# An attention block with a mixture of experts: first group normed tile by tile, routing pairs counted earlier, the last stage's first rows loaded into left buffers

## The chip, the cores and the metric

The kernel runs on one core of a Trainium2 chip. The metric is device time in microseconds (us), taken around the whole execution of the program. A core has TensorE (PE, with its weight load PEld), VectorE (DVE), ScalarE (ACT), GpSimd (POOL) and SyncE (SP). SP, ACT and POOL can also issue DMAs; an engine executes its instructions, DMA issues among them, in the order in which the program gives them.

## The reference

The input x is 4 sequences of 1024 rows of 512 floats. Everything is float32.

```python
xn = layernorm(x)                                  # no gain, no bias
q, k, v = xn @ Wq.T + bq, xn @ Wk.T + bk, xn @ Wv.T + bv      # 16 heads of 32
scores = q @ k.T / sqrt(32), causal, - slope[h] * |i - j|
attn = softmax(scores) @ v @ Wo.T + bo

logits = xn @ gate_w.T                             # 8 experts
topw, sel = top_k(softmax(logits), 2); topw /= topw.sum()
g, u = split(xn @ w1[e].T)                         # 352 wide each
expert_out[e] = (silu(g) * u) @ w2[e].T
ffn = sum over the 2 chosen experts of topw * expert_out

return x + attn + ffn
```

## The kernel before, in words

Rows are worked on in 32 tiles of 128. There are three phases on TensorE's one in-order stream.

**First phase (norm and routing, the first 105 us).** A loop of 12 steps i runs a pipeline over 8 groups of four tiles (LG = 4). `load_pair` fetches x two tiles at a time on SP's queue (the first two pairs are split in tiles between SP and ACT). `norm_stats(g)` makes mean and variance of the four tiles on DVE, `norm_root(g)` one square root for the four on ACT, `norm_rows(g)` one reciprocal on DVE and then the rows themselves: tile 0 (and tile 2 in group 0) on DVE, tile 1 on ACT, the others on POOL. `norm_turn(g)` transposes each tile on PE (L327) and ACT copies it out of PSUM (L328). `norm_gate` (L339) makes the gate's logits, `norm_top`, `norm_pick` and `norm_rank` choose the two experts of each row and count within a tile. Between these steps the loop takes pieces of the first projections from the list `proj`: four q and k pieces of the first attention unit and eight v pieces, each 8 matmuls of 512 columns; ten are used up in the loop. Before the loop, ACT issues the loads of the gate's weights (`load_gate`, L252) and of four biases (`load_consts`, L97 to L100), and then a square root on one column ("ready", L1165) with which the square root's table is loaded.

After the loop `route()` runs as six pieces, ahead of which it counts the pairs of each expert with one matmul (L447). Piece 0 makes the block table on DVE (L462 to L501); pieces 1 to 4 each build, for eight tiles, `col` and `place_` on DVE and `both` on ACT (L521 to L534), and the 16 matmuls of `fill_table` (L509) run one piece later; piece 5 makes the two experts' shares with an exponential on ACT, and the token list. Projection pieces are taken after piece 0 (two) and after piece 1 (one). Then the bias row is added into `bo_sb` (L1208), the PSUM pools are changed (`hctx.close()`), the pool of the norm phase is given back, the expert phase's first loads are issued, and the remaining three pieces of `proj` run.

**Second phase (attention and experts, to about 1500 us).** There are 16 attention units (sequence, four heads) of 12 groups. In a group PE runs `values` of the group before, `scores`, and `largest` of the next unit, then what `fill` hands it. `fill` keeps a running account: `rate` is the total weight of all fills and projections over the number of gaps, and a fill is popped while the weight spent is under `rate` times the gaps so far. Fills are the 71 expert blocks, each as a gate piece (with the transposes of the block before), an up piece and a `second_layer` piece (the down projection, `ye`, its sum with `bo_sb`, the store to `ys_d`, and the loads of the next w2). In the groups on the diagonal POOL masks the probabilities (L1013) before PE can use them in `values`.

**Third phase (the final rows, among the last two units).** `final_pieces` gives for each tile three functions: `load` fetches x again (`xr`), for the first three sequences the attention output (`ot`) from `o_d`, and two gathers of expert rows from `ys_d` by an indirect DMA that POOL issues; `piece` adds both gathered rows, weighted, into `xr` on DVE (L812), then `project` multiplies by Wo on PE (L802, 8 matmuls), adds the result on DVE (L805) and stores the row; `rest` does the projection for the last sequence. `prime` issues the loads of the first three tiles, after the expert pool has been given back; each later piece first issues the load of the tile three ahead. The buffers are four for `xr`, four for `ot` and eight for the gathered rows.

Of the kernel before, what the change touches and what calls it, by code (L numbers as in the profile page):

```python
# [28 lines left out]
def kernel(  # L29
# [17 lines left out]
    nc = tc.nc  # L47
    T, E = x.shape
# [4 lines left out]
    NC = E // P  # L53
    NT = T // P
    ST = S // P
    QB = 512
    NQ = S // QB
    QT = QB // P
# [7 lines left out]
    LG = 4  # L66
# [20 lines left out]
    eps = const.tile([P, 1], F32, tag="eps", name="eps")  # L87
# [8 lines left out]
    def load_consts():  # L96
        nc.scalar.dma_start(bq_sb, bq.rearrange("(c p) -> p c", p=P))  # L97
        nc.scalar.dma_start(bk_sb, bk.rearrange("(c p) -> p c", p=P))
        nc.scalar.dma_start(bv_sb, bv.rearrange("(c p) -> p c", p=P))
        nc.scalar.dma_start(bo_sb, bo.partition_broadcast(P))  # L100
# [12 lines left out]
    with ExitStack() as actx:  # L113
        wp = actx.enter_context(tc.tile_pool(name="wp", bufs=1))
        qkv = actx.enter_context(tc.tile_pool(name="qkv", bufs=1))
# [118 lines left out]
        xnT, qs, ks, vs, oTs, mTs = {}, {}, {}, {}, {}, {}  # L234
# [16 lines left out]
        def load_gate():  # L251
            nc.scalar.dma_start(gate_sb[:, :, :NE], gateT.rearrange("(c p) n -> p c n", p=P))  # L252
# [30 lines left out]
        def xt(t):  # L283
            return pairs[t // 2][:, t % 2, :]
# [13 lines left out]
        def norm_rows(g):  # L298
            mv, rstd = mvs.pop(g), rstds.pop(g)
            nc.vector.reciprocal(rstd, rstd)  # L300
            shift = ln.tile([P, 1], F32, tag="shift", name=f"shift{g}")
            nc.vector.scalar_tensor_tensor(
                shift, mv[:, 1, 0:1], -1.0, rstd[:, 1, :], ALU.mult, ALU.mult
            )
            for n in range(LG):
                t = xt(g * LG + n)
                if n == 1:
                    nc.scalar.activation(t, t, AF.Identity, bias=shift, scale=rstd[:, n, :])
                    continue
                eng = nc.vector if n == 0 or (g == 0 and n == 2) else nc.gpsimd  # L310
                eng.tensor_scalar(
                    t, t, mv[:, n, 0:1], rstd[:, n, :], ALU.subtract, ALU.mult
                )

        def norm_turn(g):
            b, s = g // NQ, g % NQ
# [128 lines left out]

        def route():
            nc.tensor.matmul(  # L447
                p_count, lhsT=every, rhs=ahead_[:, NT, :], start=True, stop=True, skip_group_check=True
            )

            def prefix(src, n, name):

# [321 lines left out]
        def final_pieces(b):  # L774

            held = {}

            def load(i):
                t = b * ST + i
                xr = phase["fin"].tile([P, E], F32, tag="xr" if b < B - 1 else "held", name=f"xr{t}", bufs=4 if b < B - 1 else ST)  # L780
                nc.sync.dma_start(xr, x[t * P : (t + 1) * P, :])
                o = None
                if b < B - 1:
                    o = phase["fin"].tile([P, NC, P], F32, tag="ot", name=f"ot{t}", bufs=4)
                    cols = slice((i % QT) * P, (i % QT + 1) * P)
                    nc.sync.dma_start(o, o_d[b * NQ + i // QT][:, :, cols])
                gs = []
                for j in range(TOP):
                    g = phase["fin"].tile([P, E], F32, tag="g", name=f"g{t}_{j}", bufs=8)
                    nc.gpsimd.indirect_dma_start(  # L790
                        out=g[:, :],
                        out_offset=None,
                        in_=ys_d[:, :],
                        in_offset=bass.IndirectOffsetOnAxis(ap=slot[:, j, t : t + 1], axis=0),
                    )
                    gs.append(g)
                held[i] = xr, o, gs

            def project(t, xr, lhsTs):
                y = bank([P, E], F32, name=f"y{t}")  # L800
                for c in range(NC):
                    nc.tensor.matmul(  # L802
                        y, lhsT=lhsTs[c], rhs=wo_sb[:, c, :], start=(c == 0), stop=(c == NC - 1)
                    )
                nc.vector.tensor_tensor(xr, y, xr, ALU.add)  # L805
                nc.sync.dma_start(out[t * P : (t + 1) * P, :], xr)
# [11 lines left out]
            def rest(i):  # L818
                cols = slice((i % QT) * P, (i % QT + 1) * P)
                project(  # L820
                    b * ST + i, held[i][0], [oTs[b, c, i // QT][:, cols] for c in range(NC)]
                )

            return load, piece, rest

# [251 lines left out]
        def final_all():  # L1077
            ops = [final_pieces(b) for b in range(B)]

            order = [(ops[b], i) for b in range(B - 1) for i in range(ST)]  # L1080
            for i in range(ST):
                order.insert(i * B + B - 1, (ops[B - 1], i))
            ahead = 3

            def prime():
                for ops_, i in order[:ahead]:
                    ops_[0](i)

            res = [prime]
            for k, (ops_, i) in enumerate(order):  # L1090

                def one(k=k, ops_=ops_, i=i):
# [6 lines left out]
            return res, ops[B - 1][2]  # L1099

        phase = {}

# [62 lines left out]
        nc.scalar.activation(once("ready", [P, 1]), eps, AF.Sqrt)  # L1165
# [130 lines left out]
```

## Time and profile before

| | |
|---|---|
| Runs shown | 1679.8, 1683.55, 1683.83 us; median 1683.55 us |
| Profiled execution, its own time | 1683.31 us |
| Its span, first to last instruction | 1681.6 us, 29436 instructions |
| Busy PE, DVE, ACT, POOL | 1639.1, 1008.4, 892.1, 338.8 us |
| Mean granted TensorE clock | 0.990 |
| DMA | 278.98 MB, mean 166 GB/s |

A busy share is a mean over stages with different limits. PE is busy for 97% of the span, so time is lost or won only where PE stands, and where it runs at a lower clock than granted elsewhere. In the rows of the trace, "start, us, engine line operation out<-in xcount" is followed in brackets by the idle time of the engine just before and what ended it. Rows with a "q" behind the engine's name (ACTq, SPq) are the engine's issuing of DMAs.

### The profile page before, as it was taken

How to read it: one execution, taken by the hardware profiler on the slowest of the kernel's cores; microseconds unless marked ns; L12 is line 12 of the kernel's file. 1: busy time of each engine (PE TensorE's matmuls, PEld its weight loads, DVE VectorE, ACT ScalarE, POOL GpSimd, SP SyncE). 2: the span in 40 equal slices, each digit the busy share in tenths (PEclk: the TensorE clock that was granted, in tenths of full speed). 3: DMA queues.
4: the chain of work that ended last, by engine and by line, in shares of the span. 5: the costliest groups of instructions: out<-in, count | busy, mean ns of one | idle time of the engine just before them, and what ended most of it. 6: DMA issues, size and time to landing. Idle time of an engine off the chain costs nothing.

```text
span 1681.6 us, 29436 instructions
## 1 busy us (share of the span) xinstructions
PE 1639.1 (97%) x9476; PEld 783.3 (47%) x9476; DVE 1008.4 (60%) x3136; ACT 892.1 (53%) x2074; POOL 338.8 (20%) x763
## 2 busy tenths in 40 slices
PE   7989999999999999999999999999999999989999
PEld 4545544454444444444444445445444444434333
DVE  6757656565555555565566556565655566548862
ACT  4434465554745455555646464655656474535521
POOL 5601102021110101121110202020111112035661
PEclk9989999999999999999999999999999999989999
DMA  9827655555543433556543343565443334438881
GB/s 317 316 94 245 212 181 165 182 173 188 166 126 109 124 113 123 164 172 209 169 137 99 107 159 100 183 223 190 142 130 112 122 104 157 130 119 255 261 294 63
DMA packets 146490, 278.98 MB, mean 166 GB/s; under 512 B 16448, under 2 KB 45120, under 8 KB 144800
## 3 DMA queue, kind: packets, MB, share of 16 engines
q1 hardware_dynamic: 132128, 234.60, 42.4%
q0 software_dynamic: 10800, 35.40, 7.1%
q10 hardware_dynamic: 3408, 7.10, 1.2%
q8 instruction: 75, 1.23, 0.3%
q14 instruction: 79, 0.65, 0.1%
HBM read 229.07 MB, written 47.97 MB: 165 GB/s over the span
## 4 chain that ended last, share of the span: by engine, by line
PE 93%; DVE 2%; issue 2%; DMA 1%; ACT 1%; POOL 1%; ACTq 0%; SPq 0%; DVEq 0%; POOLq 0%
PE ye L738 11%; PE pgate L690 10%; PE pup L690 10%; PE s L974 9%; PE o L1048 9%; PE m L855 8%; PE pk L584 7%; PE pv L616 7%; PE pq L584 6%; PE y L802 6%; PE s L993 2%; PE pxs L683 2%; PE pact L724 2%; DMA xg<-in_x 1%; PE ptr L327 1%
## 5 line engine op out<-in xcount | busy, mean ns | idle before, releaser
L1005 ACT ACTIVATE pr<-s,kbias 128x512 f32<-128x512 f32 (+3 forms) x768 | 382.8, 580 | 407.4 <-PE s L993 407.3
L901 ACT ACTIVATE z<-z,top 128x896 f32<-128x896 f32 (+7 forms) x512 | 391.2, 773 | 72.0 <-DVE top L891 72.0
L1013 POOL TENSOR_SCALAR_AFFINE_SELECT pr<-pr 128x128 f32<-128x128 f32 x512 | 154.8, 311 | 1135.1 <-ACT pr L1005 1128.3
L879 DVE CUSTOM_DVE_ANT_0 z<-m,rel 128x512 f32<-128x512 f32 (+3 forms) x512 | 271.5, 586 | 83.1 <-PE m L855 82.7
L738 PE MATMUL ye<-w,actT 128*128 128x512 f32 (+1 forms) x426 | 200.2, 606 | 1.7 <-issue 1.7
L690 PE MATMUL pgate<-w,xsT 128*128 128x352 f32 x568 | 184.7, 469 | 3.4 <-issue 3.1
L690 PE MATMUL pup<-w,xsT 128*128 128x352 f32 x568 | 183.1, 465 | 2.6 <-ACT pr L1005 2.6
L855 PE MATMUL m<-k,q 32*128 32x512 f32 (+3 forms) x1536 | 178.2, 489 | 5.6 <-DVE inv L1032 5.2
L974 PE MATMUL s<-q,k 32*128 32x512 f32 (+3 forms) x1536 | 178.1, 533 | 0.0
L879 DVE CUSTOM_DVE_ANT_0 z<-m,rel,l 128x128 f32<-128x128 f32 (+3 forms) x256 | 125.8, 548 | 72.9 <-PE m L855 72.9
L1048 PE MATMUL o<-pr,v 128*32 128x512 f32 (+3 forms) x1536 | 166.9, 498 | 0.6 <-POOL pr L1013 0.5
L690 PEld LDWEIGHTS pup<-w,xsT 128*128 128x128 f32 x568 | 105.0, 190 | 74.1 <-ACT pr L1005 16.0
L690 PEld LDWEIGHTS pgate<-w,xsT 128*128 128x128 f32 x568 | 104.1, 193 | 53.1 <-issue 6.0
L584 PE MATMUL pk<-xnT,wk 128*128 128x512 f32 x256 | 119.6, 610 | 4.9 <-ACT pr L1005 2.6
L616 PE MATMUL pv<-wv_sb,xnT 128*128 128x512 f32 x256 | 120.9, 618 | 0.0
L738 PEld LDWEIGHTS ye<-w,actT 128*128 128x128 f32 (+1 forms) x426 | 77.1, 192 | 90.8 <-issue 74.7
L584 PE MATMUL pq<-xnT,wq 128*128 128x512 f32 x256 | 118.1, 604 | 0.8 <-ACT pr L1005 0.8
L974 PEld LDWEIGHTS s<-q,k 32*128 32x128 f32 x1536 | 60.0, 182 | 120.6 <-issue 86.0
L855 PEld LDWEIGHTS m<-k,q 32*128 32x128 f32 x1536 | 88.9, 185 | 46.1 <-DVE oT L1063 14.0
L707 DVE SCALAR_TENSOR_TENSOR th<-th,pgate 128x352 f32<-128x352 f32 x71 | 37.0, 521 | 117.5 <-ACT th L706 117.5
L1063 DVE TENSOR_TENSOR oT<-oT,o 128x512 f32<-128x512 f32 (+3 forms) x160 | 83.8, 524 | 36.4 <-PE o L1048 35.7
L747 DVE TENSOR_TENSOR yr<-ye,bo_sb 128x512 f32<-128x512 f32 x71 | 49.1, 691 | 91.7 <-PE ye L738 91.7
(159 smaller groups left out, 1693.7 us busy)
## 6 DMA issues: line engine op xcount, KB each, us to landing
w<-in_w1T SPq DMA_DIRECT2D x284, 352.0 KB, 4.1
w<-in_w2T SPq DMA_DIRECT2D x142, 256.0 KB, 3.0
ys_d<-yr SPq DMA_DIRECT2D x71, 256.0 KB, 2.0
w<-in_w2T SPq DMA_DIRECT2D x71, 192.0 KB, 3.8
xr<-in_x SPq DMA_DIRECT2D x32, 256.0 KB, 5.6
out<-xr SPq DMA_DIRECT2D x32, 256.0 KB, 3.0
xn_d<-xT ACTq DMA_DIRECT2D x6, 1024.0 KB, 6.7
o_d<-oT SPq DMA_DIRECT2D x24, 256.0 KB, 2.5
```

Source lines behind the costliest of these rows:

```text
L584: nc.tensor.matmul(ps, lhsT=ws[which][:, i, :], rhs=xnT[b, s][:, i, :], start=(i == 0), stop=(i == NC - 1),)
L616: nc.tensor.matmul(ps, lhsT=xnT[b, t // QT][:, i, (t % QT) * P : (t % QT + 1) * P], rhs=wv_sb[:, i, :], start=(i == 0), stop=(i == NC - 1),)
L690: nc.tensor.matmul(ps, lhsT=xsT[k][:, c, :], rhs=w1s[k, c][:, gu, :], start=(c == 0), stop=(c == NC - 1),)
L738: nc.tensor.matmul(y, lhsT=a[:m, f, :], rhs=w2s.pop((k, f))[:m, :], start=(f == 0), stop=(f == NF - 1),)
L802: nc.tensor.matmul(y, lhsT=lhsTs[c], rhs=wo_sb[:, c, :], start=(c == 0), stop=(c == NC - 1))
L855: nc.tensor.matmul(pss[h][:, col : col + n], lhsT=qs[b, c, s][r, (i % QT) * P : (i % QT + 1) * P], rhs=ks[b, c, k0 // QB][r, :n], start=Tr ...
L879: nc.vector.tensor_tensor_reduce(out=zs[h][:, z0 : z0 + n], in0=pss[h][:, col : col + n], in1=rel[:, S - L + k0 : S - L + k0 + n], scale=1 ...
L901: nc.scalar.activation(z[h][:, z0 : z0 + L], z[h][:, z0 : z0 + L], AF.Exp, bias=top[:, h : h + 1], scale=-slopes[c * HC + h], accum_out=to ...
L974: nc.tensor.matmul(ps[:, :n], lhsT=ks[b, c, j // QT][r, (j % QT) * P : (j % QT + 1) * P], rhs=qs[b, c, s][r, q0:], start=True, stop=False,)
L1005: nc.scalar.activation(pr[:, :n], pss[h][:, :n], AF.Exp, bias=kbias[:, hh, d : d + 1], scale=-slopes[hh],)
L1013: nc.gpsimd.affine_select(out=pr[:, :P], in_=pr[:, :P], compare_op=ALU.is_ge, fill=0.0, base=0, pattern=[[1, P]], channel_multiplier=-1,)
L1048: nc.tensor.matmul(o[h * D : (h + 1) * D, :n], lhsT=vs[b, j][:, col : col + D], rhs=prs[h][:, :n], start=True, stop=True, skip_group_check ...
```

## The change

- **First group.** `norm_rows` no longer treats group 0, and a new `norm_first` does the first group tile by tile: statistics of one tile, its own square root on ACT, then reciprocal and rows of the tile before; even tiles on DVE, odd ones on ACT, none on POOL. `load_gate` and `load_consts` move behind it, and "ready" moves to the front of ACT's stream.
- **Counting.** The matmul that counts the pairs moves out of `route()` into the last step of the loop, ahead of that step's projection piece.
- **Routing.** A projection piece (the first k piece of the second unit) is taken after route piece 3 instead of at the start of the next phase.
- **Final rows.** `load` no longer gathers; `gather` is separate. `prime` is put before the last three expert pieces, and loads the first three tiles' x rows into the buffer of `wv` and their attention outputs into a buffer of `xnT`. A new `begin` issues the gathers of the first three tiles after the expert pool has been given back. `piece` projects alone; `join` (the two weighted adds, then the store) runs one piece later.
- **Weights.** JOIN falls from 1.5 to 0.6, and the weight of `prime` from 3.0 to 0.

```diff
-                eng = nc.vector if n == 0 or (g == 0 and n == 2) else nc.gpsimd
+                eng = nc.vector if n == 0 else nc.gpsimd
...
+        def norm_first():
+            mv = ln.tile([P, LG, 2], F32, tag="mv", name="mv0")
+            rstd = ln.tile([P, LG, 1], F32, tag="rstd", name="rstd0")
+            def stats_(n):
+                stats = ln.tile([P, 6], F32, tag="stats", name=f"stats0_{n}")
+                nc.vector.bn_stats(stats, xt(n))
+                nc.vector.bn_aggr(mv[:, n, :], stats)
+                nc.scalar.activation(rstd[:, n, :], mv[:, n, 1:2], AF.Sqrt, bias=eps)
+            def rows(n):
+                r, m = rstd[:, n, :], mv[:, n, 0:1]
+                nc.vector.reciprocal(r, r)
+                if n % 2 == 0:
+                    nc.vector.tensor_scalar(xt(n), xt(n), m, r, ALU.subtract, ALU.mult)
+                    return
+                shift = ln.tile([P, 1], F32, tag="shift", name=f"shift0_{n}")
+                nc.vector.scalar_tensor_tensor(shift, m, -1.0, r, ALU.mult, ALU.mult)
+                nc.scalar.activation(xt(n), xt(n), AF.Identity, bias=shift, scale=r)
+            stats_(0)
+            for n in range(1, LG):
+                stats_(n)
+                rows(n - 1)
+            rows(LG - 1)
...
-        def route():
+        def count_pairs():
             nc.tensor.matmul(
                 p_count, lhsT=every, rhs=ahead_[:, NT, :], start=True, stop=True, skip_group_check=True
             )
+        def route():
...
-            def load(i):
+            def load(i, xr=None, o=None):
...
+            def gather(i):
...
             def piece(i):
+                xr, o = held[i][:2]
+                if o is not None:
+                    project(b * ST + i, xr, [o[:, c, :] for c in range(NC)])
+            def join(i):
                 t = b * ST + i
-                xr, o, gs = held[i]
+                xr, o, *gs = held[i]
                 for j in range(TOP):
                     nc.vector.scalar_tensor_tensor(
                         xr, gs[j], share[:, t, j : j + 1], xr, ALU.mult, ALU.add
                     )
                 if o is not None:
-                    project(t, xr, [o[:, c, :] for c in range(NC)])
+                    store(t, xr)
...
             def prime():
-                for ops_, i in order[:ahead]:
-                    ops_[0](i)
+                o = qkv.tile([P, NC, QB], F32, tag="xnT", name="ot_first", bufs=2)
+                xr = wp.tile([P, NC, E], F32, tag="wv", name="xr_first")
+                for n, (op, i) in enumerate(order[:ahead]):
+                    op[0](i, xr[:, n, :], o[:, :, n * P : (n + 1) * P])
+            def begin():
+                for op, i in order[:ahead]:
+                    op[1](i)
...
                     if k + ahead < len(order):
                         nxt, ni = order[k + ahead]
                         nxt[0](ni)
-                    ops_[1](i)
+                        nxt[1](ni)
+                    op[2](i)
+                    if k > 0:
+                        order[k - 1][0][3](order[k - 1][1])
+                    if k + 1 == len(order):
+                        op[3](i)
...
-        PROJ, JOIN = 3.6, 1.5
-        fills = [(0.0, begin_experts)] + expert_pieces() + [(0.0, begin_final), (3.0, finals[0])]
-        fills += [(JOIN if k % B == B - 1 else PROJ, f) for k, f in enumerate(finals[1:])]
+        PROJ, JOIN = 3.6, 0.6
+        fills = [(0.0, begin_experts)] + expert_pieces()
+        fills.insert(len(fills) - 3, (0.0, finals[0]))
+        fills += [(0.0, begin_final), (0.0, finals[1])]
+        fills += [(JOIN if k % B == B - 1 else PROJ, f) for k, f in enumerate(finals[2:])]
...
-        load_gate()
-        load_consts()
+        nc.scalar.activation(once("ready", [P, 1]), eps, AF.Sqrt)
         set_qscale()
         bqs = const.tile([P, NC], F32, tag="bqs", name="bqs")
-        nc.scalar.activation(once("ready", [P, 1]), eps, AF.Sqrt)
...
         for i in range(GR + 4):
-            if 1 <= i <= GR:
+            if i == 0:
+                norm_first()
+                load_gate()
+                load_consts()
+                continue
+            if 2 <= i <= GR:
                 norm_rows(i - 1)
...
+            if i == GR + 3:
+                count_pairs()
...
-            for _ in range((2, 1)[i] if i < 2 else 0):
+            for _ in range((2, 1, 0, 1, 0, 0)[i]):
                 proj.pop(0)()
```

More of the change, by code (lines that the diff above doesn't have):

```diff
@@ L776, in final_pieces @@
             held = {}
-            def load(i):
+            def load(i, xr=None, o=None):
                 t = b * ST + i
-                xr = phase["fin"].tile([P, E], F32, tag="xr" if b < B - 1 else "held", name=f"xr{t}", bufs=4 if b < B - 1 else ST)
+                if xr is None:
+                    xr = phase["fin"].tile(
+                        [P, E],
+                        F32,
+                        tag="xr" if b < B - 1 else "held",
+                        name=f"xr{t}",
+                        bufs=4 if b < B - 1 else ST,
+                    )
                 nc.sync.dma_start(xr, x[t * P : (t + 1) * P, :])
-                o = None
                 if b < B - 1:
-                    o = phase["fin"].tile([P, NC, P], F32, tag="ot", name=f"ot{t}", bufs=4)
+                    if o is None:
+                        o = phase["fin"].tile([P, NC, P], F32, tag="ot", name=f"ot{t}", bufs=4)
                     cols = slice((i % QT) * P, (i % QT + 1) * P)
                     nc.sync.dma_start(o, o_d[b * NQ + i // QT][:, :, cols])
-                gs = []
+                held[i] = xr, o
+            def gather(i):
+                t = b * ST + i
                 for j in range(TOP):
@@ L795, in load @@
                     )
-                    gs.append(g)
-                held[i] = xr, o, gs
+                    held[i] += (g,)
             def project(t, xr, lhsTs):
@@ L805, in project, with store @@
                 nc.vector.tensor_tensor(xr, y, xr, ALU.add)
+            def store(t, xr):
                 nc.sync.dma_start(out[t * P : (t + 1) * P, :], xr)
             def piece(i):
+                xr, o = held[i][:2]
+                if o is not None:
+                    project(b * ST + i, xr, [o[:, c, :] for c in range(NC)])
+            def join(i):
                 t = b * ST + i
-                xr, o, gs = held[i]
+                xr, o, *gs = held[i]
                 for j in range(TOP):
@@ L815, in piece @@
                 if o is not None:
-                    project(t, xr, [o[:, c, :] for c in range(NC)])
+                    store(t, xr)
             def rest(i):
+                t = b * ST + i
                 cols = slice((i % QT) * P, (i % QT + 1) * P)
[L820 to L824, printed above, removed]
+                project(t, held[i][0], [oTs[b, c, i // QT][:, cols] for c in range(NC)])
+                store(t, held[i][0])
+            return load, gather, piece, join, rest
         M_GROUPS = []
@@ L1085, in prime, with one @@
             def prime():
-                for ops_, i in order[:ahead]:
-                    ops_[0](i)
-            res = [prime]
-            for k, (ops_, i) in enumerate(order):
-                def one(k=k, ops_=ops_, i=i):
+                o = qkv.tile([P, NC, QB], F32, tag="xnT", name="ot_first", bufs=2)
[5 more added lines that the diff above has]
+                    op[1](i)
+            res = [prime, begin]
+            for k, (op, i) in enumerate(order):
+                def one(k=k, op=op, i=i):
                     if k + ahead < len(order):
@@ L1095, in one @@
                         nxt[0](ni)
-                    ops_[1](i)
+                        nxt[1](ni)
[4 more added lines that the diff above has]
+                        op[3](i)
                 res.append(one)
-            return res, ops[B - 1][2]
+            return res, ops[B - 1][4]
         phase = {}
```

## The prediction

> **What bounds the kernel now.** I read the page's chain of work that ended last and its clock row, then the waits and the timeline of the three stretches that the change touches, then tables of short windows for the clock.
>
> ```profile
> PE 93%; DVE 2%; issue 2%; DMA 1%; ACT 1%; POOL 1%; ACTq 0%; SPq 0%; DVEq 0%; POOLq 0%
> PEclk9989999999999999999999999999999999989999
> ```
>
> PE sets the end, so an edit is worth what it takes out of PE's idle time or of PE's slow time. The clock row has two dips, in the 3rd and the 36th slice of 42 us (84 to 126, 1471 to 1513), and the change works in both. The start, by the timeline:
>
> ```profile
> 4.90 0.38 ACTq L98 DMA_DIRECT2D bk_sb<-in_bk  x1
> 6.50 1.28 ACT L1165 ACT_TABLE_LOAD   x1 [6.50 <-DMA xg<-in_x]
> 10.49 0.59 ACT L328 COPY xnT<-ptr 128x512 f32<-128x512 f32 x1 [0.88 <-PE ptr L327]
> 12.71 0.69 DVE L290 BATCH_NORM_STATS2 stats<-xg 128x6 f32<-128x512 f32 x1 [2.74 <-DMA xg<-in_x]
> 16.04 0.30 ACT L296 ACTIVATE rstd<-mv,eps 128x4 f32<-128x4 f32 x1 [2.64 <-DVE mv L291]
> 21.09 0.66 PE L327 MATMUL ptr<-ident,xg 128*128 128x128 f32 x4 [1.40 <-POOL xg L311]
> ```
>
> ACT is busy issuing loads until 6.5 us. The second group's x reaches DVE only at 12.71, its square root runs at 16.04, POOL's two tiles end at 21.04, and PE waits for them. From there to 64 us the chain is PE without a gap, so what moves 21.09 moves all that follows. The handover to the experts:
>
> ```profile
> 79.82 0.42 DVE L462 TENSOR_TENSOR more<-routing,steps 128x256 f32<-128x256 f32 x1 [3.95 <-PE routing L447]
> 87.90 1.26 ACT L528 ACTIVATE both<-col,iota_col 128x1136 bf16<-128x1136 bf16 x1 [0.55 <-DVE col L521]
> 98.34 1.26 ACT L528 ACTIVATE both<-col,iota_col 128x1136 bf16<-128x1136 bf16 x1 [0.51 <-DVE col L521]
> 104.83 5.23 PE L584 MATMUL pk<-xnT,wk 128*128 128x512 f32 x8 [2.28 <-issue]
> ```
>
> PE idles here because DVE and ACT build the table; a k piece that takes 3.60 elsewhere takes 5.23. The last stage, PE's waits from 1480 us on (total, times, longest), all above 0.3 us:
>
> ```profile
> PE y L802 <- DMA ot<-o_d: 4.0, 1, 4.0
> PE ye L738 <- issue: 1.7, 1, 1.7
> PE m L855 <- DVE inv L1032: 1.2, 1, 1.2
> PE o L1048 <- POOL pr L1013: 0.5, 1, 0.5
> ```
>
> and windows of 2 us (busy PE, PEld, DVE, ACT, POOL with counts, then granted clock, DMA share, GB/s):
>
> ```profile
> 1490.00:1492.00 2.00, 1.47 (x6) 0.47 (x3) 2.00 (x8) 0.00 (x0) 0.27 (x1) 0.59 0.00 0
> 1502.00:1504.00 2.00, 0.00 (x0) 0.00 (x0) 1.82 (x7) 1.54 (x5) 0.99 (x3) 1.00 0.61 183
> 1504.00:1506.00 2.00, 0.68 (x1) 0.50 (x2) 0.00 (x0) 0.00 (x0) 1.39 (x3) 0.51 0.97 292
> 1506.00:1508.00 2.00, 2.00 (x3) 0.67 (x2) 0.00 (x0) 0.00 (x0) 1.70 (x2) 0.50 0.69 178
> ```
>
> The clock is half after each of the waits.
>
> **First group.** DVE does four statistics at a pitch of 0.79, four reciprocals at some 0.2, two tiles of 0.54 and two shifts of 0.16: 5.4 us from 4.73, so it ends at 10.1 and ACT's last tile (0.81) at about 11.1; POOL's tile ended at 11.02 before. "Ready" in front is covered, since its table load (1.28) now runs while x is still on its way. But ACT then issues five loads before it copies the first transposes: 0.45, 0.58, 0.38, 0.52 and 0.46 by the rows of the old issues, 2.4 us, to 13.6. Four copies of 0.59 to 0.60 end at 16.0, where they ended at 13.39. Queued behind them on ACT is the second group's square root: 16.0 instead of 16.04, so the earlier x of that group (SP's third load waited until 6.23, held 3.5 us by x and then by the small loads) is worth nothing. PE does the gate's matmuls (1.07), the q piece (3.70) and 16 transposes (1.79) from 16.05: 22.6 instead of 21.75. **+0.9 us.** From below: if the issues hid entirely, POOL's chain could begin when DVE's statistics end (10.1 + 3.2 = 13.3 against 16.0) and PE gain 2.1 with q in between: -2.1. From above: the old five issues lay among waits of 2.3 us in all (2.82 to 4.90, and 0.2 ahead of L100), and now many more loads are in flight; twice these waits make +0.9 + 4.6 = +5.5. I take the issues without waits: the loads that they would wait for have had 10 us to land, and the old ones landed in 4 to 7.
>
> **Counting and the k piece.** Counted ahead of a projection piece, the pairs are known 3.5 us earlier. But in ACT's order `both` stands behind the copy of the second v piece, which ends at 87.35, so it begins at 87.4 instead of 87.90: 0.5 us. PE then goes through the first table part, the bias row and the second table part to about 95.6, and the k piece (3.43) to 99.1 in what was idle. Its copy on ACT (0.69) stands ahead of the last `both`, which therefore begins at 99.9 instead of 98.34: 1.6 us late, and with it all that leads to PE's restart (104.83 becomes 106.4). The cover is DVE's and ACT's work on the table; without it the piece would cost its 3.43 at once. In return one cold piece is gone: the q piece that ended at 113.49 ends at 106.4 + 5.23 = 111.6. **-1.9 us.** Ends: -3.7 if the clock is not halved (3.43 for 5.23), +1.6 if the experts' loads, issued 1.6 later, set the end; against that, the first expert matmul (121.68) waited for DVE's copy behind four L879, not for a load.
>
> **Final rows.** The first y no longer waits: 3.99 us of idle go, and 6.41 - 3.63 = 2.78 of half clock: -6.8. The weights fall by 8 x 0.9 + 3.0 = 10.2 of 1020.7; going through `fill` with both lists, the last expert piece moves two groups on (from the first to the third of unit 14), and two full expert pieces stand where the last block's transposes waited for DVE. I take the 1.72 of idle before the last `ye` as gone and half of its half-clock loss (4.80 - 2.74 = 2.06): -2.7. `prime`'s six loads stand on SP ahead of the store of block 69 and the w2 of block 70, at six times 0.34 to 0.63: 3 us of issue that ends before that store is due, at a DMA share of 0.16 and less.
>
> Where does the wait go? `begin` puts six gathers on POOL at a pitch of 1.25 us, and the masks of the next, diagonal, group stand behind them. From the end of `ye`, the store lands 3.4 later (1497.99 to 1501.38), the gathers take 7.5 to 11.1, four masks of 0.28 go to 12.2. PE meanwhile has `values` and `scores` (1.12) and two y pieces: 8.5. It waits 3.7 in `values`, about what it waited for `ot`. The half clock after it: between the 2.78 behind a wait of 3.99 and the 1.7 of the first pgate (4.26 for 2.58, behind 3.10); I take 1.7, since PE comes from 8.5 us of full work. +5.4. **Sum of this part -4.1.** Ends: -9.5 without the new wait, +5 with joins that hold POOL (below).
>
> On the clock the rows say that 1.20 us of idle within some 3 us was enough for 0.59. The Trainium skill, "TensorE: Matmul & The Clock Gate", Part 1, says that the clock halves only after an idle window of about 3.4 us. By that rule, which differs from the row, a kernel that keeps only the short wait of 1.20 would pay no half clock there, and the part would be 1.0 better. The skill's "SBUF — State Buffer" ("SBUF: two separate sides") speaks against the change: descriptors of a POOL DMA are held up while DVE runs in a two-port mode; the 64 gathers took 0.942 to 1.412 here, so at most 0.47 each, and by the rule the joins could cost more.
>
> **Sum.** 0.9 - 1.9 - 4.1 = -5.1, against the profiled execution's 1683.31 (span 1681.6 and 1.7 around it; 0.24 under the median): **1678 us**.
>
> **Rivals.** *The new wait is hidden* (the gathers start later than the masks, or PE has more queued): -5.1 - 5.4 = -10.5, 1673. For it: POOL's gathers already waited 18.7 us for L812, and PE for POOL only 0.5. Against: the order on POOL is fixed.
>
> *ACT is held at the start.* The five issues wait as bk's did: +4.6, 1683, no change. For it: the gap before 4.90. Against: see above.
>
> *Masks behind joins, slower.* A gather needs a buffer that the join frees, and the join now follows the next y. After a y's end: add 0.69, join 1.54, two gathers 2.5, masks 1.2: 5.9 us, where PE has `values`, `scores` and a y, 5.5. Ten diagonal groups lie in the stage. At 0.4 each this is 4; DVE late by 1 us makes 14 and 1692, and above 0.5 per group the whole gain is gone. For it: DVE is busy 17 of 20 us from 1540 to 1600. Against: unit 15 has no L879, so DVE is free there. I price it at 1689.
>
> **Chances.** The sum holds (1674 to 1682): 0.38. Hidden wait: 0.19. ACT held: 0.21. Masks behind joins: 0.22. About 0.3% (5 us) is what a measurement of this kernel can tell from no change; the sum's own case falls on both sides of 1678.5. Faster: 0.24 + 0.19 = 0.43; same: 0.14 + 0.21 = 0.35; slower: 0.22. Range 1669 to 1689; the sum's own case 1674 to 1682.
>
> **What would show it.** Right: ACT copies of the first group behind five issues, ending near 16; `more` near 77; the last `both` near 100; PE's first y directly behind `scores`, at full clock, and then a wait of PE for POOL L1013 of 3 to 4 us. Wrong: PE's stream behind 21 us late by more than 2; waits of PE for POOL at many diagonal groups; no wait at all behind the first gathers.

## The result and the profile after

The changed kernel takes 1704.37 us (median of four runs, 1702.33 to 1706.31); the kernel before, in runs beside them, 1683.69. The ratio is 1.0122, with a 95% interval of 1.0109 to 1.0135: **20.7 us slower**, where 1678 was forecast and 1689 was the upper end. The profiled execution has a span of 1704.6 us (own time 1706.31), 23.0 above the span of before.

The page of after: its clock row and its chain by engine.

```profile
PEclk9999999999999999999999999999999999999999
PE 90%; DVE 3%; DMA 3%; issue 1%; ACT 1%; POOL 1%; ACTq 0%; SPq 0%; POOLq 0%; DVEq 0%
```

The chain has lost three points of PE, and DMA has gone from 1% to 3%: that is already where to look. The clock row hides more than it shows: no slice of 43 us falls under 9, since the waits are now scattered.

**The start.** Timeline of after, 10 to 24 us:

```profile
11.97 2.56 ACTq L100 DMA_DIRECT2D bo_sb<-in_bo  x1
14.58 2.05 ACT L355 COPY xnT<-ptr 128x512 f32<-128x512 f32 x4 [3.90 <-issue]
16.49 0.33 ACT L296 ACTIVATE rstd<-mv,eps 128x4 f32<-128x4 f32 x1
16.68 1.93 PE L366 MATMUL plg<-xnT,gate 128*32 128x512 f32 x8 [4.84 <-ACT xnT L355]
18.55 4.31 PE L613 MATMUL pq<-xnT,wq 128*128 128x512 f32 x8
22.70 1.91 PE L354 MATMUL ptr<-ident,xg 128*128 128x128 f32 x16
```

The five issues stand where the prediction put them, between the norm and the copies, but the last took 2.56 us and not 0.46. The copies end at 16.6 (16.0 forecast), and PE, after 4.84 us of idle, does the gate's matmuls in 1.93 (1.07 before) and q in 4.31 (3.70). The second group's transposes end at 24.61; 21.75 was before, 22.6 forecast.

**The handover.** Timeline of after, 79 to 115 us:

```profile
79.17 0.42 DVE L491 TENSOR_TENSOR more<-routing,steps 128x256 f32<-128x256 f32 x1 [0.46 <-PE routing L474]
98.28 3.64 PE L613 MATMUL pk<-xnT,wk 128*128 128x512 f32 x8
102.55 1.25 ACT L557 ACTIVATE both<-col,iota_col 128x1136 bf16<-128x1136 bf16 x1
109.07 5.11 PE L613 MATMUL pq<-xnT,wq 128*128 128x512 f32 x8 [2.81 <-DVE bo_sb L1274]
```

The k piece runs in what was idle, and PE is back at full work at 114.2 where it was at 113.5: 0.7 late after a start that was 2.85 late, so this part brought 2.1.

**The last stage.** PE's waits from 1480 us on (total, times, longest), those above 1.0 us:

```profile
PE o L1094 <- POOL pr L1059: 7.8, 7, 3.6
PE y L841 <- DMA ot<-o_d: 4.1, 3, 3.3
PE m L901 <- DVE oT L1106: 1.6, 1, 1.6
PE m L901 <- DVE inv L1078: 1.2, 1, 1.2
```

and PE's timeline at the first y pieces:

```profile
1510.91 3.70 PE L841 MATMUL y<-wo_sb,ot_first 128*128 128x512 f32 x8
...
1514.66 3.60 PE L841 MATMUL y<-wo_sb,ot_first 128*128 128x512 f32 x8
1521.83 1.35 PE L1094 MATMUL o<-pr,v 128*32 128x128 f32 x8 [3.57 <-POOL pr L1059]
```

The first y stands directly behind the scores, at full speed, and the wait behind it is 3.57 (3.7 forecast). Up to here the forecast's mechanism is in the trace.

To see what follows, I take the start of each group's exponents (L1005 before, L1051 after) and subtract the filling work that the two orders place differently ahead of it, each piece at its mean duration. What is left is how late the changed kernel stands against before (us; "14.2" is unit 14, group 2):

| | 14.0 | 14.2 | 14.4 | 14.6 | 14.10 | 15.0 | 15.4 | 15.8 | 15.11 |
|---|---|---|---|---|---|---|---|---|---|
| after | 7.7 | -2.3 | 3.8 | 6.3 | 7.7 | 14.8 | 18.2 | 22.3 | 23.0 |

Three things stand in this row. From 14.0 to 14.2 the changed kernel gains 10.0. From 14.2 to 14.4 it loses 6.1, the wait for the masks and the half clock behind it. And then it loses 19.2 us more, in the 29 pieces that the prediction's sum did not look at. It also comes into the stage 7.7 late, where 0.7 came out of the handover; the subtraction is approximate inside the middle stage (two orders at different points), but the last column is the difference of the spans.

The later loss shows first on SP, whose waits the prediction never read for this stage. The one row of before and that of after for the same wait (x rows waiting for a store), from 1500 us on:

```profile
SPq L781 <- DMA out<-xr: 1.7, 2, 1.5
```

```profile
SPq L818 <- DMA out<-xr: 55.5, 17, 5.3
```

and SP's timeline of after in the worst place:

```profile
1637.41 0.35 SPq L847 DMA_DIRECT2D out<-xr  x1
1637.83 5.99 SPq L818 DMA_DIRECT2D xr<-in_x  x2
1643.92 0.53 SPq L823 DMA_DIRECT2D ot<-o_d  x1
1644.55 0.56 SPq L847 DMA_DIRECT2D out<-xr  x1
1650.42 0.33 SPq L818 DMA_DIRECT2D xr<-in_x  x1
1650.84 0.53 SPq L823 DMA_DIRECT2D ot<-o_d  x1
...
1656.74 3.70 PE L841 MATMUL y<-wo_sb,ot 128*128 128x512 f32 x8 [3.27 <-DMA ot<-o_d]
```

With four buffers, the x row of a tile goes where the row of four y pieces earlier lay, and cannot be loaded before that row is stored. The store is now issued with the join, one piece later, just ahead of the load that waits for it. SP goes in order, so the load of `ot`, whose own buffer is long free, stands behind that wait: a round of store and load takes 6 to 7 us here, and PE waits for `ot` at the end of it.

The ring of gathered rows shows on POOL. Its waits of gathers for joins, before and after:

```profile
POOL g L790 <- DVE xr L812: 18.7, 13, 6.3
POOL g L830 <- DVE xr L858: 44.7, 18, 5.7
```

The largest step of the table, 7.1 us from 14.10 to 15.0, holds a wait of this kind:

```profile
1577.09 1.34 POOL L830 DMA_INDIRECT g<-ys_d,slot  x1 [3.96 <-DVE xr L858]
...
1581.15 1.34 POOL L830 DMA_INDIRECT g<-ys_d,slot  x1 [1.47 <-DVE xr L858]
...
1586.66 1.77 PE L1094 MATMUL o<-pr,v 128*32 128x256 f32 x8 [2.57 <-POOL pr L1059]
```

The gathers wait for joins, the masks of the group stand behind four gathers, and PE waits 2.57 us for them. PE then works at a granted clock of 0.50 in the two windows of 2 us from 1588 on.

### The profile page after: what moved, and what is told of

It reads as the page before. It is cut to its first block, busy times and chain, and to the rows that moved or that the text cites. A ratio compares the mean times of both kernels' runs of the same rounds, so it can differ in the third digit from the quotient of the medians.

```text
span 1704.6 us, 29426 instructions
## 1 busy us (share of the span) xinstructions
PE 1647.9 (97%) x9476; PEld 786.6 (46%) x9476; DVE 1007.2 (59%) x3140; ACT 891.5 (52%) x2078; POOL 337.9 (20%) x762
## 4 chain that ended last, share of the span: by engine, by line
PE 90%; DVE 3%; DMA 3%; issue 1%; ACT 1%; POOL 1%; ACTq 0%; SPq 0%; POOLq 0%; DVEq 0%
PE ye L767 11%; PE pup L719 10%; PE pgate L719 10%; PE s L1020 9%; PE o L1094 8%; PE m L901 8%; PE pv L645 7%; PE pq L613 7%; PE pk L613 7%; PE y L841 4%; PE pxs L712 2%; PE s L1039 2%; PE pact L753 2%; DMA out<-xr 1%; POOL g L830 1%
## 5 line engine op out<-in xcount | busy, mean ns | idle before, releaser
L1051 ACT ACTIVATE pr<-s,kbias 128x512 f32<-128x512 f32 (+3 forms) x768 | 381.9, 579 | 425.2 <-PE s L1039 417.3
L1094 PE MATMUL o<-pr,v 128*32 128x512 f32 (+3 forms) x1536 | 171.2, 500 | 7.8 <-POOL pr L1059 7.8
```

The costliest lines, as they stand in the source:

```text
L1051: nc.scalar.activation(pr[:, :n], pss[h][:, :n], AF.Exp, bias=kbias[:, hh, d : d + 1], scale=-slopes[hh],)
L1094: nc.tensor.matmul(o[h * D : (h + 1) * D, :n], lhsT=vs[b, j][:, col : col + D], rhs=prs[h][:, :n], start=True, stop=True, skip_group_check ...
```

## The experiments

Ratios are to the kernel before in runs on the same chip, with 95% intervals; one thousandth is 1.7 us.

### Each part alone

**The first group alone** (`norm_first`, the loads behind it, "ready" in front; the rest as before).

> The kernel before with the first part alone (first group normed tile by tile, the gate's and constants' loads behind it). Both theories read the trace of after, where the second group's first transposes end 2.85 us later than before (24.61 against 21.75). Theory 'the last stage loses it all': the delay is carried to the end, 1683.7 + 2.9 = 1686.6 (1685 to 1688). Rival 'a late start grows in the middle' (the shift between the two traces goes from +0.7 at 189 us over -7.5 at 614 us to +7.7 at 1482 us): 1690 or more.

Measured: 1.0021 (1.0004 to 1.0038), some 3.5 us. In the trace the second group's transposes end at 24.84 (before 21.75) and the kernel comes into the last stage 3.7 late. A loss that is carried on: 4.0 late at 189 us, 2.2 in the middle, 3.7 at 1482. This one execution ends 11.5 late; what its last stage adds does not show in the ratio.

**Counting and the k piece alone.**

> The kernel before with the second part alone (pairs counted ahead, one k piece put between the table's parts). By the traces the gain of this part is what is left of the shift at the handover: +0.7 there less +2.85 from the start, -2.1: 1681.6 (1680 to 1683). Rival 'it only changes which loads collide in the middle': anything from 1678 to 1690, and the q pieces behind the handover end no earlier than 113.5 us.

Measured: 0.9979 (0.9961 to 0.9996). Against before, the start of each group of the middle is early by 1.85 us, from 189 to 1482 us without a change of more than 0.02. This part does what it should.

**The final rows alone** (all functions of the last stage, and the weights).

> The kernel before with the third part alone (first rows in left buffers, joins one piece later, the weights of the filling order). Theory 'the last stage loses it all': the shift falls by 10 us at the stage's begin and climbs by 25 us behind it, so +15 to +21: 1699 to 1705. Rival 'the loss comes from the three parts together' (late start, then loads that collide): 1690 or less.

Measured: 1.0094 (1.0065 to 1.0123), 15.9 us. So the loss is in this part, and the three parts alone (1.0021, 0.9979, 1.0094) add up to 1.0094, near the 1.0122 of all.

### What in the final rows costs

**Joins in their own piece again**, behind their y:

```
                     op[2](i)
-                    if k > 0:
-                        order[k - 1][0][3](order[k - 1][1])
-                    if k + 1 == len(order):
-                        op[3](i)
+                    op[3](i)
```

> The changed kernel with each piece's join and store in its own piece again, behind its y (not one piece later). Theory 'late joins': the stores, and with them the buffers for x rows and gathered rows, come one piece earlier, so the waits of the late stage (25 us in all) shrink to a few and the gain at the first y stays: 1704.4 less 15 to 22, 1682 to 1689. Rival 'weights and order': the pieces stand where the filling put them, and no wait goes: 1701 to 1707. A third: the first join, on DVE ahead of all that follows, waits for the first gathers (about 12 us behind the last ye), and PE stands behind DVE there: 1690 to 1698.

Measured: 1.0017 (1.0003 to 1.0031): 10 thousandths of the 12 go by putting the join, and with it the store, one piece earlier. SP's wait of x rows for stores is down to 2.1 us there. The weights are not the whole of it, then. The wait for the masks behind the first gathers is still there (4.2).

**The weights alone, on the kernel before** (`PROJ, JOIN = 3.6, 0.6` for 1.5, and 0.0 for 3.0).

> The kernel before with only the weights of the filling order changed as in the change (joins 0.6 for 1.5, priming 0 for 3.0): every fill stands a little later, no instruction differs. Theory 'the order itself costs': in the traces of after, of the third part alone and of joins in their own piece, PE's waits between 130 and 1480 us are 4.4 to 6 us above before (PE for ACT in pup, PE for a load of xnT), and the shift grows by 7 to 12 us there, so +4 to +9 us before the last stage, and in all a ratio of 1.002 to 1.006. Rival 'the shift in the middle is a fault of the accounting': PE's waits between 130 and 1480 us as before, ratio 0.999 to 1.001.

Measured: 1.006 (1.0043 to 1.0077), 10 us, with no instruction changed: the upper end of the first theory. Part of it is the middle (PE's waits there are 14.6 us for 10.1), and part the last stage, whose first y waited 6.3 for `ot` where 4.0 was before; the rest was not traced wait by wait. Two of PE's largest waits between 130 and 1480 us, before:

```profile
PE m L855 <- DVE inv L1032: 4.1, 4, 1.2
PE pup L690 <- ACT pr L1005: 2.6, 4, 0.8
```

and with only the weights changed:

```profile
PE pup L690 <- ACT pr L1005: 5.5, 7, 1.1
PE m L855 <- DVE inv L1032: 5.3, 5, 1.2
```

A lower sum of weights puts the expert pieces at other groups, and there `pup` meets ACT's exponents seven times and not four.

**More buffers.** The last block's eight x rows are put into left buffers (an `xnT`, the three `wqk`, `bv_rows`), and the room goes to x rows (four to six), to gathered rows (eight to twelve), or to both:

```
-  xr: tag="xr" if b < B - 1 else "held", bufs=4 if b < B - 1 else ST
+  xr: room.pop(0) if b == B - 1, else tag="xr", bufs=6
-  g:  bufs=8
+  g:  bufs=12
```

> The changed kernel with six buffers for the rows of x in the place of four (the last block's eight held rows lie in left buffers). Theory 'late stores': loads no longer wait for the store of the piece just joined; the waits of PE for o rows (4.1) and what SP's order holds back go, some 8 to 14 us: ratio to before 1.004 to 1.008, against 1.0122. Rival 'masks behind joins': the gathered rows still have eight buffers, the masks still stand behind gathers that wait for joins: ratio 1.010 to 1.013.

> The changed kernel with twelve buffers for gathered rows in the place of eight, x rows left at four. Theory 'masks behind joins': gathers don't wait for the last join any more, masks come in time, PE's waits for POOL after the first (7.8 less 3.6) and their half clock go, 8 to 12 us: ratio 1.005 to 1.008. Rival 'late stores': x rows and the o rows queued behind them are as late as before: ratio 1.010 to 1.013.

> The changed kernel with both (six buffers for x rows, twelve for gathered rows). Theory 'one piece later costs buffers, and nothing else': the late stage loses no more than the wait behind the first gathers (5 to 6): of 25 us 15 to 19 go, ratio 1.001 to 1.003. Rival 'the work of the stage is bound otherwise' (16 DMA engines at a share of 0.8 to 0.9, or DVE): at most half of it goes, ratio 1.006 or more.

Measured: six for x rows 1.0082 (1.0065 to 1.0099); twelve for gathered rows 1.0151 (1.0129 to 1.0173), worse than the change itself; both 1.0049 (1.0033 to 1.0066). With six for x rows alone, PE still waits for POOL as often as in the change (the 2.57 of 1586 is 2.58 there):

```profile
PE o L1098 <- POOL pr L1063: 7.8, 7, 3.6
```

With twelve for gathered rows alone, POOL's later waits are gone, and PE waits for o rows instead (SP's wait for stores has grown to 65.5):

```profile
PE y L845 <- DMA ot<-o_d: 13.4, 10, 4.2
PE o L1098 <- POOL pr L1063: 3.6, 1, 3.6
```

With both, no wait for `ot` is left:

```profile
PE o L1098 <- POOL pr L1063: 4.1, 3, 3.6
```

So the two rings together were too short for a join one piece later. Neither theory foresaw that longer gathered rows alone make things worse; why gathers that run further ahead lengthen the wait for stores (55.5 to 65.5) wasn't tried by itself.

### What is left with the buffers

**The weights of before, with both buffers.**

> The changed kernel with six buffers for x rows, twelve for gathered rows, and the weights of before (1.5 for a join, 3.0 at the first gathers). With the new weights this kernel stood at 1.0049. Theory 'the order costs by itself': the weights alone cost 1.006 on the kernel before; PE's waits between 130 and 1480 us fall from 14.5 to about 10 us and the ratio falls by 0.003 to 0.006, to 0.999 to 1.002. Rival 'the new weights cost only where joins stand in their piece': 1.004 to 1.006.

Measured: 1.0033 (1.002 to 1.0045), 1.6 thousandths better than with the new weights, less than expected, and the two intervals overlap. PE's waits in the middle are 10.0 us, as before (10.1; the change has 14.7).

**The first gathers inside the first piece**, so that on POOL they stand behind the masks of that group (the change's weights, both buffers).

> The changed kernel with those buffers, its own weights, and the first six gathers issued inside the first piece, so that on POOL they stand behind the masks of that group and not ahead of them. Theory (the prediction's step 'masks behind six gathers', 3.7 of wait and 1.7 of half clock): the first wait of PE for POOL (3.58 at 1517.5) goes, ratio 1.0049 less 0.002 to 0.0033, 1.0016 to 1.003. Rival 'the wait moves': join 0 now waits for its rows on DVE, and PE waits for DVE by as much: 1.004 to 1.006.

Measured: 1.0027 (1.0017 to 1.0036), 2.2 thousandths better: the wait of 3.6 and the half clock after it go, and no wait for DVE takes their place there. The two intervals just touch; the trace is the better evidence.

**Counting, final rows, both buffers, the weights of before, the first gathers in the first piece; the first group as before.**

> The kernel before with the second and third parts, the buffers, the weights of before and the first gathers inside the first piece; the first group as before. Sum of the pieces measured: counting -0.0021, first y without its wait about -0.004 to -0.006, no new wait, no cost of the order: 0.992 to 0.996. Rival 'the wait at the first y was cover for something else' (the order of the stage, loads at a share of 0.8 to 0.9): 0.997 to 1.001.

Measured: 1.0012 (1.0002 to 1.0022). A miss: no gain at all. It stood 8.0 ahead of before at 14.2 and 2.3 behind at 14.10. Two of PE's waits, and the first of them in the timeline:

```profile
PE o L1071 <- POOL pr L1036: 2.9, 2, 2.5
PE m L878 <- DVE oT L1086: 2.1, 2, 1.6
```

```profile
1512.55 1.79 PE L1071 MATMUL o<-pr,v 128*32 128x256 f32 x8 [2.53 <-POOL pr L1036]
```

With the old weights one y stands in this group and not two, so the masks of the next group come sooner behind the eight gathers. And the join behind each y keeps DVE from `oT`, for which PE's next work waits.

**The loads in front again, for the first part alone.**

> The first part alone on the kernel before, with the loads of the gate and the constants in front of everything again. Theory 'ACT is held by its five issues behind the first group': without them the copies end where they did or earlier, the second group's chain starts at the arrival of its x as before, ratio 0.999 to 1.001 (against 1.0021 for the part as it was). Rival 'the tile by tile norm itself is slower, on DVE and ACT': 1.0015 to 1.003. In the trace: the first transposes of the second group begin at 21.0 to 21.8 us by the theory, at 23.5 to 25 by the rival.

Measured: 1.0013 (1.0003 to 1.0023), with the interval across both theories. In the trace the second group's transposes begin at 20.93, but all 16 in a row, and end at 22.84 (21.75 before). At this point of the trace some two thirds of the part's loss is the five issues (24.84 to 22.84 of the 3.09 us); the rest is the norm itself: the first square root comes at 7.84, behind the table load, the copies end at 14.5 (13.4 before), and the gate takes 1.93 again, here behind only 0.81 us of idle.

### A version that is faster than both

**Join ahead of the next y, nothing else** (on the change):

```
-                    op[2](i)
                     if k > 0:
                         order[k - 1][0][3](order[k - 1][1])
+                    op[2](i)
```

> The changed kernel with one thing moved: the join of piece k-1 stands ahead of the y of piece k on DVE, not behind it; buffers, weights and gathers as in the change. Theory 'the order on DVE holds the buffers': the join no longer waits for the next y, so x rows, stores and gathered rows come free a y (3.6) earlier, and DVE has no join to do between a y and the next group: of the late stage's 25 us 12 to 18 go, ratio 1.002 to 1.006. Rival 'four and eight buffers are too few one piece later, wherever the join stands': 1.009 to 1.012.

Measured: 1.0106 (1.0089 to 1.0123). The first theory missed: SP's wait for stores is 70.9 us there. With four and eight buffers the place of the join on DVE alone does not help.

**Gathers spread and join ahead of y**, on the kernel of 1.0012: the gathers of one tile in the first piece, of two in each of the second and third, then of one a piece.

> The kernel before with the counting, the early rows, six and twelve buffers, the weights of before; the first gathers spread (one tile in the first piece, two in the second and third, then one a piece) and each join ahead of the next y. The kernel without these two things stood at 1.0012: it gained 6.6 at the first y and gave back 10 by waits of PE for POOL's masks behind eight gathers (2.5 and half clock) and for DVE behind joins (1.6 twice). Theory 'these two waits ate the gain': 4 to 8 us less, 0.996 to 0.998. Rival 'another wait takes their place, or the stage is bound by its loads': 0.999 to 1.002.

Measured: **0.9933 (0.9916 to 0.9949)**, 1673.33 us beside 1683.95: 11 us faster than before. PE's waits from 1480 us on are down to three rows:

```profile
PE ye L740 <- issue: 2.1, 1, 2.1
PE m L878 <- DVE inv L1055: 1.2, 1, 1.2
PE m L878 <- DVE oT L1086: 0.3, 1, 0.3
```

and a window of 20 us (busy PE, PEld, DVE, ACT, POOL, clock, DMA share, GB/s) shows that the DMA engines, at a share of 1.04, were not what held the stage:

```profile
1600.00:1620.00 20.00, 20.00 (x93) 7.27 (x91) 11.60 (x18) 7.99 (x15) 15.66 (x19) 1.00 1.04 359
```

**The first y ahead of the last `ye`**, to fill the wait of 2.1:

> As the last, with the first y (it needs no gathered row) put ahead of the last ye, where PE waits 1.9 us for the transposes of the last block and works at half clock behind it. Theory: the wait and its half clock (2.1) go: 2 to 4 us below the last kernel. Rival 'the wait moves to the store of the last block, so the gathers and the first joins are 3.7 later': within 1 us of the last kernel, or above it.

Measured: 0.9953 (0.9936 to 0.9969), no better; the wait for `ye` goes, but at 14.5 both kernels stand alike (7.1 and 7.0 ahead), with a new wait of 1.8 for DVE's `oT` and 0.8 for POOL.

Then each of three things was taken back from the best kernel. On that chip the kernel before itself took 1685.5 to 1694.8, so the ratios are less sharp, and the best kernel wasn't run beside them; their traces say which wait comes back.

> The best kernel so far (0.9933) with each join behind the next y again; gathers spread as there. Theory 'the spread gathers did it': PE's wait for masks is gone with them, the joins cost only the two waits for DVE (1.6 each): 0.9945 to 0.9965. Rival 'the joins behind y did it': back to 0.9985 to 1.0015.

Joins behind y: 1.002 (1.0006 to 1.0034). PE waits for DVE again, 2.3 for the add of `xr` among them:

```profile
PE m L878 <- DVE xr L821: 2.3, 1, 2.3
...
PE m L878 <- DVE oT L1086: 1.9, 2, 1.3
```

> The best kernel so far with four buffers for x rows and eight for gathered rows as before. Theory 'one piece later needs more buffers': loads of x rows and o rows wait for stores again, though the join is a y earlier than in the change, and gathers are asked for only two pieces ahead: 0.997 to 1.003. Rival 'with the join ahead of y and gathers two ahead, four and eight are enough': 0.993 to 0.995.

Four and eight buffers: 1.0011 (0.9994 to 1.0029). SP's wait for stores is back at 47.6 and PE's for `ot` with it:

```profile
PE y L814 <- DMA ot<-o_d: 8.0, 5, 3.1
```

PE waits for DVE there as well: 2.9 for a join, 1.9 for the add of an x row and 1.7 for `oT`; the last two stand at 1529 to 1532, with half clock behind them.

> The best kernel so far with the weights of the change (0.6 and 0 for 1.5 and 3.0). Theory 'the order costs by itself', +4 to +7 us in the middle (PE's waits for ACT in pup 5.5 for 2.6, one for a load of xnT): 0.996 to 0.999. Rival 'the weights cost only where the last stage was short of buffers': 0.992 to 0.994.

The change's weights: 1.009 (1.006 to 1.0121), far above both expectations. PE's waits in the middle are 14.4 again, and in the last stage four gathers, the first at 1612.09 after POOL had waited 2.98 us for DVE, run ahead of the masks of a group, and PE waits 2.55. PE also waits 7.7 us once for ACT, at 1634, and ACT stood 18.4 us before that for something that the profile doesn't name; so how much of the 1.009 is the order, and how much this, stays open.

```profile
1615.86 0.95 POOL L807 DMA_INDIRECT g<-ys_d,slot  x1 [0.30 <-DVE inv L1055]
1616.81 1.03 POOL L1036 TENSOR_SCALAR_AFFINE_SELECT pr<-pr 128x128 f32<-128x128 f32 x4
```

```profile
1617.17 1.12 PE L1071 MATMUL o<-pr,v 128*32 128x128 f32 x8 [2.55 <-POOL pr L1036]
```

In all three, by these ratios, taking one thing back loses all or nearly all of the 11 us, so they are not gains that add. The spread of the gathers was not taken back by itself.

## Why the prediction was wrong

**First group: +0.9 forecast, +2.85 in the trace, 3.5 (0.7 to 6.4) alone.** Inside its bounds, and the mechanism (ACT held by its issues) was right for some two thirds of it. Mis-sized was the fifth issue (2.56 for 0.46; "I take the issues without waits" was the wrong choice of the two), though the copies ended only 0.6 later than forecast. The larger miss is PE's speed, which was not a term of the sum: gate, q and transposes take 7.93 us (16.68 to 24.61) where the prediction has 6.55, at the durations that they had in the kernel before. The last section shows it.

**Counting and the k piece: -1.9 forecast, -2.1 in the trace, -3.5 (-6.6 to -0.7) alone.** Right, by its own steps: k in the idle time, the last `both` late by what the k copy and the start put ahead of it, one cold piece less.

**Final rows: -4.1 forecast, +15.9 (10.9 to 20.7) alone.** This is the step that failed, not in its terms but in where it stopped. The terms up to the first new wait came out: from 14.0 to 14.4 the balance is -3.9 for -4.1, with +5.4 where the table has 6.1. That -6.8 and -2.7 make 9.5 where the table has 10.0 at 14.2 is partly luck: the changed kernel has not come to its first y there, and a new wait of 1.0 us for w2 stands ahead of its last `ye`. What was left out:

- *The other 29 pieces were counted at nothing.* The prediction saw that a gather needs a buffer that the join frees, put it into a rival, and priced it from POOL and DVE alone (5.9 us against PE's 5.5, 0.4 a group). It never asked the same of x rows: four buffers, a store one piece later, SP in order with the loads of `ot` behind. The runs show the two rings as the larger half: six buffers for x rows and twelve for gathered ones take 1.0122 to 1.0049, some 12 of the 20.7 us; six alone take it to 1.0082, twelve alone make it worse.
- *"The weights fall by 10.2"* was read for what it does at the last two expert blocks. It moves every piece behind the first: 1.006 by itself, on the kernel before. How much depends on the rest, since with both buffers it was 1.6 thousandths.

**The rivals.** "Masks behind joins, slower" had the right sign and one of the two rings; its price, 1689, was 15 too low. "The new wait is hidden" is out: 3.57 in its place. "ACT is held at the start" was right in kind, with 2.1 us on one issue for its +4.6.

**Clock.** The Trainium skill, "TensorE: Matmul & The Clock Gate", Part 1, asks for an idle window of about 3.4 us before the clock halves. The traces show less: in the changed kernel, after a wait of 1.20 us (to 1488.83), 0.74 and then 0.50 were granted in the two windows of 2 us from 1490 on, and eight `pgate` matmuls took 4.22 us (2.58 at full clock); in the kernel of 1.0012, after 2.53 us of waiting, it was 0.79 and then 0.50 from 1512 on. The prediction went by its rows there, and was right to, but of a half-clock loss of 2.06 it counted half as gone where 1.64 stayed.

**The port that DVE shares with POOL.** That DVE holds up the descriptors of POOL's DMAs, which the prediction took from the skill's "SBUF — State Buffer" ("SBUF: two separate sides") and weighed against the joins, does not show here: 64 gathers have a median of 0.946 us before, 0.947 after and 0.947 in the fastest kernel, where joins lie at three different places, and the longest takes 1.41, 1.41 and 1.36. Whether a DVE instruction here runs in a two-port mode, the traces don't say.

## What to carry to other kernels

A step that is moved one place later lengthens the life of every buffer it frees: count, for each ring it touches, how many pieces lie between the load that needs a buffer and the instruction that frees it, and read the waits of the queue that issues those loads, above all when it goes in order and other loads stand behind. Weights of a filling order are an edit to the whole kernel, not to the pieces they name. And where a gain of 10 us is seen to arrive and be lost again, take back one thing at a time: here longer rings and the join ahead of the next y both had to hold before 0.9933 was there, with the weights of before and the gathers spread; what the spread is worth alone is not shown.

## Not expected of the hardware

- A store of 256 KB (`out<-xr`) took 2.04 us to land at 1570 us and 5.86 to 6.06 at 1637 to 1657, where loads and gathers filled the DMA engines at a share of 0.84; a ring that does at 2 us is too short at 6. The share around 1570 (1570 to 1573) was 0.57.
- Eight gate matmuls took 1.93 us at 16.68 us and 1.07 at 13.45 us in the kernel before, though the granted clock reads 1.00 in both windows. That 1.00 is no reading: the clock record in the trace begins at 12.40 us before, at 18.46 with the first group alone and its loads in front, and at 19.81 after, and PE's speed changes at just these times. Before, a transpose takes 0.42 us up to 12.4 and 0.27 from there on; after, a q matmul takes 1.22 at 18.55 and 0.59 from 20.1 on. Norming tile by tile brings PE its first work 2.2 us earlier (7.20 for 9.36) but broken by idle, and PE comes to full speed 7.4 us later.
- With the counting alone, PE's stream keeps its distance of 1.85 us to before within 0.02 us over 1300 us. Shifts between two traces are a measurement here, until the last stage, where loads decide.
